# A post-norm decoder layer on one core: both batches share weights in the attention and one output projection

## The chip, the core and the metric

The kernel runs on one core of a Trainium2 chip. The time is that of one execution on the device, in microseconds (us). The kernel before ran three times: 1895.61, 1897.80 and 1900.67 us, median 1897.8. A further execution was recorded by the hardware profiler; its own time, from the first to the last instruction, is called the span.

The engines that appear below: TensorE (PE; its weight loads are shown apart as PEld), VectorE (DVE), ScalarE (ACT), GpSimd (POOL) and SyncE (SP), which issues nearly all transfers. Each engine works through its own instructions in order, and a transfer that waits for its room holds back those behind it on SP.

## The reference

Two batches of 512 tokens with 1024 features each go through one layer (cut to what is computed):

```python
def attention(x, wq, wk, wv, wo):           # 32 query heads, 8 key/value heads, 128 wide
    q, k, v = x @ wq.T, x @ wk.T, x @ wv.T  # split into heads, 4 query heads share one k and v
    s = q @ k.T / sqrt(128)                 # masked: j <= i and i - j < 128
    return (softmax(s) @ v) @ wo.T          # 4096 features back to 1024

def cross(x, ctx):                          # ctx: 2 x 1024 x 1024
    fake = lambda a, s, z: (clip(round(a / s + z), 0, 255) - z) * s
    return fake(x, s1, z1) @ fake(ctx, s2, z2)

def ffn(x):                                 # ternary weights, 2752 wide
    inter = silu(x / 128 @ w_gate.T) * (x / 128 @ w_up.T)
    q = int8(trunc(clip(inter * 128, -128, 127)))
    return int8(trunc(clip(q @ w_down.T * 128, -128, 127)))

x = layernorm(x + attention(x))
x = layernorm(x + cross(x, ctx[b]))
x = layernorm(x + ffn(x))
```

## The kernel before

**Arithmetic.** The f32 products are done with one level of Strassen and Winograd's form: seven products of half-size blocks in place of eight, with sums of blocks made by DVE. A product of f32 with 256 columns is two PE instructions, which follow each other 216 ns apart, so 0.432 us in the profile. A pair of heads of one batch costs 28 such products in `strassen` (L132), 12.1 us. The sums of the weights' blocks are made by `strassen_left` (L112 to L115: four DVE operations on 128x512), those of the activations, once for a batch, by `strassen_right`.

**Attention.** `attention` goes through 16 groups: the eight key/value heads of batch 0, then the eight of batch 1. A group takes three pairs of projections: key and value, then query heads 0 and 1, then 2 and 3. So each weight pair is loaded (L240) and summed twice, once for each batch. While a group's four tiles of 128 tokens are attended to, the projections of the next group run between the steps, `STEPS = 6` calls of `other` for one tile. A tile ("row" below) is: two score matmuls (`ps`, L338), copies and mask (L348 to L352), the row's maximum (L359), `exp` (L362), its reciprocal (L367), the multiplication that makes the weights (L368), transposes on PE (`pt`, L374), copies, and the matmuls `o` (L395 to L398), whose result goes into `factors` (L401). `keep` makes the Strassen sums of `factors` and stores them in DRAM as `kept` (L424).

**Background.** Generators stand in lists and are advanced a step at a time by `in_attention`: `ahead` makes the weights' sums of the output projection and the FFN and stores them in DRAM (`wo_sums`, `sums`); from batch 1 on, `behind` runs the output projection of batch 0 and `aside` its cross tokens.

**Output projection.** `project_out(b)` is made once for each batch. Its 56 steps go through seven products k in the order 1, 2, 6, 7, 4, 5, 3, and for each k through eight groups g. One step takes the seven sums of `kept` (`ol`, 448 KB, L483) and the weights (`or`, 512 KB, L490; from `wo` for k up to 3, from `wo_sums` above), makes four DVE sums of the latter (`right_sums`, L502, L503, L504 and L507: 128x256) and does seven products of 256 columns (L563, 3.02 us). After g = 7 of a k, `read` adds the products to the residual rows `xres` (L524 to L530). The loads for the weights are issued three steps ahead, those of `ol` two ahead.

**Cross attention.** `Cross.context(b)` reads the context in eight tiles of 512 KB: a load into the one buffer of `b_raw` (L635), three DVE operations (`quantise`, L615, L620, L621), and one ACT operation (`whole`, L625) which writes the tile as bf16. `constants` loads four parameters ahead of this (L597) and takes reciprocals of them. `tokens(b)` does the layernorm of four tiles, their product with the context, and the second layernorm.

**FFN.** 22 units of 128 features for batch 0, then 22 for batch 1. Between the units of batch 0 stand the output projection of batch 1 (1020 to 1334 us), its context and its tokens.

**Order.** The tile framework keeps each engine's instructions in the order of the program unless a planner moves them; `keep_in_program_order` pins one. PSUM before: two banks for projections, four for `y`, one for scores, one for transposes.

Of the kernel before, what the change touches and what calls it, by code (L numbers as in the profile page):

```python
# [18 lines left out]
P = 128  # L19
B = 2  # L20
# [26 lines left out]
SLOT = {1: 0, 2: 1, 3: 6, 4: 3, 5: 4, 6: 5, 7: 2}  # L47

# [39 lines left out]
def strassen_right(nc, pool, x, name):  # L88


    factors, steps = strassen_right_steps(nc, pool, x, name)
    for step in steps:
        step()
    return factors


def strassen_right_steps(nc, pool, x, name):

    b11, b12, b21, b22 = (x[:, ts(k, KH), ts(n, NH)] for k in range(2) for n in range(2))
    t = pool.tile([P, 4, KH, NH], F32, tag="t", name=name)  # L100
    t1, t2, t3, t4 = (t[:, k] for k in range(4))
    less = lambda *which: lambda: nc.vector.tensor_tensor(*which, ALU.subtract)
    return (b11, b21, b22, t4, t1, t2, t3), (less(t1, b12, b11), less(t2, b22, t1), less(t3, b22, b12), less(t4, b21, t2))
# [15 lines left out]
def strassen(nc, spaces, work, left, right, outs, name, sums=None):  # L119

# [11 lines left out]
    def bank(k):  # L135
        return spaces[k // 2].tile([P, NH], F32, tag="p", name=f"prod{k}_{name}")

    if sums is None:
        sums = [work.tile([P, NH], F32, tag=f"st{k}", name=f"st{k}_{name}", bufs=1) for k in range(3)]
    p1, u2, u3 = sums  # L140
# [5 lines left out]
    nc.vector.tensor_tensor(u2, two, p1, ALU.add)  # L146
    yield
    roomy = spaces[0] is not spaces[1]
    if roomy:
        three = bank(2)  # L150
        product(three, 5, True)
        yield
# [4 lines left out]
    nc.vector.tensor_tensor(u3, two, p1, ALU.add)  # L157
    yield
    if roomy:
        nc.vector.tensor_tensor(c22, like(three), like(u3), ALU.add)  # L160
        four = bank(3)
        product(four, 4, True)
        nc.vector.tensor_tensor(c21, like(four), like(u3), ALU.add)
        yield
    else:
        three = bank(2)
        product(three, 5, True)
        nc.vector.tensor_tensor(c22, like(three), like(u3), ALU.add)
        yield
        product(two, 4, False)  # L170
        nc.vector.tensor_tensor(c21, like(two), like(p1), ALU.add)
        yield
    product(three, 3, False)
    nc.vector.tensor_tensor(c12, like(three), like(u2), ALU.add)
# [6 lines left out]
class Background:  # L181
# [20 lines left out]

    def drain(self):
        while self.queue:
            for _ in self.queue.pop(0)[0]:
                pass


def attention(nc, tc, consts, xbuf, tpool, wpool, ps_p, ps_y, dram, kept, complete, between):

# [3 lines left out]
    with ExitStack() as ctx:  # L217
# [8 lines left out]
        groups = [(b, g) for b in range(B) for g in range(NKV)]  # L226
        STEPS = 6

        PAIRS = 1 + G // 2
        order = [(b, g, j) for b, g in groups for j in range(PAIRS)]  # L230
        weights, lefts, right = {}, {}, {}

        def load_weight(n):
            if n >= len(order):
                return
            _, g, j = order[n]
# [6 lines left out]
        def prepare(n):  # L243
            if n < len(order):
                lefts[n] = strassen_left(nc, tc, wpool, weights[n], f"s_{n}")

        def load_x(b):
            xT = xbuf.tile([P, KC, N], F32, tag=f"x{b}", name=f"xT{b}")
# [9 lines left out]
            return xT  # L258

        weights[0] = wpool.tile([P, 2, KC, P], F32, tag="w", name="w_0")  # L260
        x0 = load_x(0)
        load_weight(1)

        qT, kT, vT, v, vd = {}, {}, {}, {}, {}

        def project_first(outs):

            ps = [ps_p.tile([P, N], F32, tag="p", name=f"first{h}") for h in range(2)]
            for c in range(KC):

                for k, part in enumerate((ts(0, NH), ts(1, NH)) if c == 0 else (slice(None),)):
                    for h in range(2):
                        nc.tensor.matmul(  # L273
                            ps[h][:, part], weights[0][:, h, c], x0[:, c, part],
# [4 lines left out]
            load_weight(2)  # L279
            prepare(1)  # L280
            right[0] = strassen_right(nc, tpool, x0, "t_0")

        def project(n):

            b, g, j = order[n]
            if j == 0:
                c1 = kT[b, g] = kvpool.tile([P, N], F32, tag="kT", name=f"kT_{n}")
                c2 = vT[b, g] = kvpool.tile([P, N], F32, tag="vT", name=f"vT_{n}", bufs=1)
# [4 lines left out]
            if n == 0:  # L293
                project_first((c1, c2))
                yield
                return
            outs = [c[:, ts(half, c.shape[1] // 2)] for c in (c1, c2) for half in range(2)]
            for k, _ in enumerate(strassen(nc, (ps_p, ps_y if b == 0 else ps_p), work, lefts.pop(n), right[b], outs, n)):
                if k == 4:
                    prepare(n + 1)  # L300
                elif k == 6:
                    load_weight(n + 2)
                yield LUMP if k == 4 else None

        def transpose_v(b, g):
# [3 lines left out]
            v[b, g] = kvpool.tile([P, TPB, P], F32, tag="v", name=f"v_{b}_{g}")  # L309
            nc.scalar.copy(v[b, g], ps)  # L310
            vd[b, g] = kvpool.tile([P, TPB - 1, P], F32, tag="vd", name=f"vd_{b}_{g}")
            nc.vector.tensor_tensor(vd[b, g], v[b, g][:, 1:], v[b, g][:, : TPB - 1], ALU.subtract)

        def pieces(m):

            b, g = groups[m]
            for j in range(PAIRS):
                yield from project(m * PAIRS + j)
                if j == 0:
                    transpose_v(b, g)  # L320
                    yield
# [109 lines left out]
        for _ in pieces(0):  # L431
            pass
        pending, late = None, []
        for m, (b, g) in enumerate(groups):
            if m + 2 == NKV:
                x1 = load_x(1)
            if m + 1 == NKV:

                right[1], late = strassen_right_steps(nc, tpool, x1, "t_1")
                late = list(late)  # L440
                for _ in range(2):
                    late.pop(0)()
            rest = pieces(m + 1) if m + 1 < len(groups) else iter(())
            for i in range(TPB):

                def other():
                    lump = next(rest, None)
                    if late:
                        late.pop(0)()
                        lump = LUMP  # L450
                    between(b, g, i, lump, keeping)

                s = scores(b, g, i, other)
                weigh(pending, other)
                pending = b, g, i, s
                for _ in range(STEPS - 2):
                    other()
            for _ in rest:
                pass
# [4 lines left out]
def project_out(nc, tc, b, xres, spaces, psum, kept, complete, wo_d, sums, x_d, begun):  # L464

    respool, stream = spaces  # L470
    LAST = NKV - 1


    grow = {1: (True, ((0, 1), (1, 0), (1, 1))), 2: (False, ((0, 0),)), 6: (True, ((0, 1),)),
            7: (False, ((1, 1),)), 4: (False, ((1, 0),)), 5: (True, ((1, 1),)), 3: (False, ((0, 1),))}
    steps = [(k, g) for k in grow for g in range(NKV)]
    lefts, rights, factors = {}, {}, {}

    def load_left(n):
        if n < len(steps):  # L480
            k, g = steps[n]
            lefts[n] = stream.tile([P, 7, P], F32, tag="left", name=f"ol_{b}_{n}", bufs=3)
            nc.sync.dma_start(out=lefts[n], in_=kept[:, g, SLOT[k]])  # L483

    def load_right(n):
        if n < len(steps):
            k, g = steps[n]
            rights[n] = stream.tile([P, 2, 2, HQ], F32, tag="right", name=f"or_{b}_{n}")
# [3 lines left out]
    def right_sums(n):  # L492

# [6 lines left out]
        t = stream.tile([P, 3, HQ], F32, tag="sums", name=f"ot_{b}_{n}", bufs=2)  # L500
# [14 lines left out]
    while b and not begun[0]:  # L515
        yield
# [3 lines left out]
    banks = [psum.tile([P, 2, HQ], F32, tag="p", name=f"y{k}_{b}") for k in range(4)]  # L520

    places = {1: (0, 0), 6: (0, 1), 7: (1, 0), 2: (2, 0), 3: (2, 1), 4: (3, 0), 5: (3, 1)}
    order = list(places)

    def read(k):
        w = stream.tile([P, 4, HQ], F32, tag="right", name=f"yw_{b}_{k}")
        p1, u4, u2, u3 = (w[:, j] for j in range(4))
        q1, q6, q7, q5 = banks[0][:, 0], banks[0][:, 1], banks[1][:, 0], banks[3][:, 1]
# [6 lines left out]
        grown = banks[2], banks[3]  # L535
# [4 lines left out]
        for n, (h, e) in enumerate(grow[k][1]):  # L540
            for q in range(2):
                block = x[:, 2 * h + q, ts(e, HALF)].rearrange("p (e c) -> p e c", e=2)
# [6 lines left out]
    for n, (k, g) in enumerate(steps):  # L549
        while n + 2 < len(steps) and (b, steps[n + 2][1], "kept") not in complete:  # L550
            yield
        if n == NKV - 4:
            while b and (b - 1, "tokens") not in complete:
                yield
            x = respool.tile([P, TPB, D], F32, tag="xres", name=f"xres{b}")
            for i in range(TPB):
                nc.sync.dma_start(out=x[:, i], in_=x_d[ts(b * TPB + i, P), :])
                xres[b * TPB + i] = x[:, i]
        left, mine, sums_now = lefts.pop(n), factors.pop(n), following
        for part in (order[:4], order[4:]):  # L560
            for j in part:
                bank, half = places[j]
                nc.tensor.matmul(  # L563
                    banks[bank][:, half], left[:, SLOT[j]], mine[j],
                    start=grow[k][0] and g == 0 and half == 0, stop=g == LAST, skip_group_check=True,
                )
# [665 lines left out]
```

## Time and profile before

| | |
|---|---|
| runs, us | 1895.61, 1897.80, 1900.67; median 1897.8 |
| span of the profiled execution, us | 1894.7 |
| mean granted PE clock | 0.998 |
| PE instructions (matmuls, transposes) | 8678 |
| bytes moved by DMA | 416.88 MB, 220 GB/s mean |
| read from / written to HBM | 318.77 MB / 96.47 MB |
| longest wait of PE | 3.6 us, for the first tile of `xT` at the start |

How it is read: an engine's busy time is given beside its share of the span. A line of 40 digits shows the busy share of each fortieth of the span in tenths, 9 for 90% or more; PEclk is the clock granted to PE in tenths of full speed. The chain that ended last is the chain of work followed back from the last instruction. A group of instructions is given as line, engine, operation, output<-inputs, partitions x elements. For a transfer the profile shows where it was issued and when it landed.

### The profile page before, as it was taken

The numbers are of one execution on the slowest core, as the hardware profiler recorded it, in microseconds if no ns is written. First come the engines' busy times: TensorE is split into PE (matmuls) and PEld (weight loads), VectorE is DVE, ScalarE is ACT, GpSimd is POOL, SyncE is SP. The second block draws the span as 40 slices with busy tenths as digits, with TensorE's granted clock in tenths as the row PEclk, the third lists the DMA queues.
The fourth block names the chain that finished last, engine by engine and source line by source line (L and its number), as shares of the span: only waits on it lengthen the run. The fifth ranks groups of instructions, "written<-read, shape, count | busy, mean of one in ns | idle before, by whom it ended". The sixth has DMA issues, their size and how long they took to land.

```text
span 1894.7 us, 24665 instructions
## 1 busy us (share of the span) xinstructions
PE 1871.1 (99%) x8678; PEld 1547.8 (82%) x8678; DVE 1370.2 (72%) x3021; ACT 563.5 (30%) x1571; POOL 13.7 (1%) x32
## 2 busy tenths in 40 slices
PE   9999999999999999999999999999999999999997
PEld 6888888878888888888777888888787778888885
DVE  4678888887777676768787667766876787655657
ACT  1334433332221221233543111212233254321224
POOL 0000000000000000000000000000000000000000
PEclk9999999999999999999999999999999999999999
DMA  8478888777888888856367777766344245643431
GB/s 310 169 264 287 289 279 279 269 246 252 281 297 275 283 276 290 280 189 211 122 211 277 270 274 251 268 234 221 122 150 149 86 150 178 200 138 132 167 130 45
DMA packets 183323, 416.88 MB, mean 220 GB/s; under 512 B 16672, under 2 KB 93728, under 8 KB 183200
## 3 DMA queue, kind: packets, MB, share of 16 engines
q1 hardware_dynamic: 181760, 412.94, 63.3%
q10 hardware_dynamic: 1440, 2.36, 0.4%
q8 instruction: 69, 1.13, 0.2%
q14 instruction: 54, 0.44, 0.1%
HBM read 318.77 MB, written 96.47 MB: 219 GB/s over the span
## 4 chain that ended last, share of the span: by engine, by line
PE 86%; DVE 7%; DMA 3%; ACT 2%; issue 1%; SPq 0%; DVEq 0%; ACTq 0%
PE prod L132 51%; PE y L563 16%; PE d L819 7%; PE ps L338 3%; PE o L397 2%; PE o L398 2%; PE m L687 1%; PE pt L374 1%; PE first L273 1%; PE o L395 1%; ACT s L362 1%; DMA ol<-kept 1%; PE rest L811 1%; DMA wd<-in_wd_dram 1%; DVE factors L409 0%
## 5 line engine op out<-in xcount | busy, mean ns | idle before, releaser
L563 PE MATMUL y<-or,ol 128*128 128x256 f32 x896 | 243.4, 379 | 1.3 <-DMA ol<-kept 1.2
L563 PEld LDWEIGHTS y<-or,ol 128*128 128x128 f32 x896 | 169.1, 190 | 27.9 <-issue 3.2
L563 PE MATMUL y<-ot,ol 128*128 128x256 f32 x672 | 184.3, 383 | 1.4 <-DVE ot L507 1.1
L132 PE MATMUL prod<-xT,w 128*128 128x256 f32 x752 | 182.9, 380 | 0.1
L132 PE MATMUL prod<-t,w 128*128 128x256 f32 x752 | 177.0, 379 | 0.0
L132 PE MATMUL prod<-t,s 128*128 128x256 f32 x752 | 176.9, 379 | 0.1
L132 PE MATMUL prod<-x2T,wgu 128*128 128x256 f32 x672 | 160.2, 379 | 0.0
L132 PEld LDWEIGHTS prod<-t,s 128*128 128x128 f32 x752 | 140.3, 190 | 23.6 <-issue 5.5
L132 PEld LDWEIGHTS prod<-xT,w 128*128 128x128 f32 x752 | 139.4, 190 | 24.3 <-issue 6.7
L132 PEld LDWEIGHTS prod<-t,w 128*128 128x128 f32 x752 | 140.1, 190 | 23.2 <-issue 6.2
L132 PE MATMUL prod<-t,wgu 128*128 128x256 f32 x672 | 158.2, 379 | 0.0
L132 PE MATMUL prod<-t,sgu 128*128 128x256 f32 x672 | 155.7, 379 | 0.7 <-ACT g L154 0.5
L563 PEld LDWEIGHTS y<-ot,ol 128*128 128x128 f32 x672 | 124.7, 190 | 27.5 <-DVE ot L507 6.2
L132 PEld LDWEIGHTS prod<-t,sgu 128*128 128x128 f32 x672 | 127.2, 190 | 19.4 <-ACT g L154 0.9
L132 PEld LDWEIGHTS prod<-t,wgu 128*128 128x128 f32 x672 | 127.3, 190 | 18.6 <-issue 0.5
L132 PEld LDWEIGHTS prod<-x2T,wgu 128*128 128x128 f32 x672 | 127.4, 190 | 17.9 <-issue 0.5
L362 ACT ACTIVATE s<-s,top 128x128 f32<-128x128 f32 x256 | 99.6, 391 | 37.8 <-DVE top L359 37.0
L819 PE MATMUL d<-hi,act 128*128 128x512 f32 x256 | 108.1, 422 | 0.0
L348 ACT COPY s<-ps 128x128 f32<-128x128 f32 x192 | 39.5, 231 | 229.0 <-PE ps L338 228.9
L833 DVE TENSOR_TENSOR acc<-d,acc 128x512 f32<-128x512 f32 x104 | 71.6, 691 | 44.6 <-PE d L819 44.1
L819 PE MATMUL d<-lo,act 128*128 128x512 f32 x256 | 101.3, 396 | 0.0
L157 DVE TENSOR_TENSOR st<-prod,st 128x256 f32<-128x256 f32 x89 | 37.6, 422 | 81.2 <-PE prod L132 81.0
(220 smaller groups left out, 2985.8 us busy)
## 6 DMA issues: line engine op xcount, KB each, us to landing
kept<-factors SPq DMA_DIRECT2D x112, 448.0 KB, 3.5
ol<-kept SPq DMA_DIRECT2D x112, 448.0 KB, 5.2
w<-in_wq_dram SPq DMA_DIRECT2D x64, 512.0 KB, 4.7
or<-wo_sums SPq DMA_DIRECT2D x64, 512.0 KB, 5.1
sgu<-sums SPq DMA_DIRECT2D x42, 768.0 KB, 6.4
or<-in_wo_dram SPq DMA_DIRECT2D x48, 512.0 KB, 4.5
wgu<-in_wgu_dram SPq DMA_DIRECT2D x42, 512.0 KB, 3.9
wd<-in_wd_dram SPq DMA_DIRECT2D x42, 512.0 KB, 3.6
```

The source lines that it names most:

```text
L132: nc.tensor.matmul(ps, left[k - 1][:, c, :], right[k - 1][:, c, :], start=start and c == 0, stop=c == KH - 1, skip_group_check=True)
L157: nc.vector.tensor_tensor(u3, two, p1, ALU.add)
L273: nc.tensor.matmul(ps[h][:, part], weights[0][:, h, c], x0[:, c, part], start=c == 0 and k == 0, stop=c == KC - 1, skip_group_check=True,)
L338: nc.tensor.matmul(ps[:, k, cut // BLOCK : G + 1].rearrange("p d w -> p (d w)"), qT[b, g][:, G * i + c].rearrange("p h w -> p (h w)"), kT[ ...
L348: nc.scalar.copy(s[:, c, c * BLOCK :], ps[:, k, : G - c].rearrange("p d w -> p (d w)"))
L362: nc.scalar.activation(s[:, h, :], s[:, h, :], AF.Exp, bias=top[:, h : h + 1], scale=QSCALE, accum_out=total[:, h : h + 1],)
L374: nc.tensor.transpose(ps[:, :, ts(c, BLOCK)], s[:, c, :], ident)
L397: nc.tensor.matmul(ps, v[b, g][:, i - 1, :], both, start=True, stop=False)
L398: nc.tensor.matmul(ps, vd[b, g][:, i - 1, :], cur, start=False, stop=True)
L563: nc.tensor.matmul(banks[bank][:, half], left[:, SLOT[j]], mine[j], start=grow[k][0] and g == 0 and half == 0, stop=g == LAST, skip_group_ ...
L819: nc.tensor.matmul(ps, act[:, ts(i, P)], half[:, part], start=start and k == 0, stop=stop and k == len(parts) - 1)
L833: nc.vector.tensor_tensor(acc[t][:, ts(e, HALF)], ps, acc[t][:, ts(e, HALF)], ALU.add)
```

## The change

**Attention.** The loop goes over the eight heads outside and the two batches inside. `sets` lists for each head which pair of which batch is projected when: pair 0 of both, pair 1 of batch 0, pair 2 of batch 0, and then, while batch 0's rows are attended to, pairs 1 and 2 of batch 1. A weight pair is loaded once and summed once and stays until both batches have used it. Both batches' activations are loaded at the start, and both sums of them made there. The number of calls for a row is 5 for batch 0 and 8 for batch 1 (`STEPS = (5, 8)`). Of the background only `ahead` remains in the attention (a step for three calls, before four), and in the last group (batch 1, head 7) steps of the output projection for every second call.

**Output projection.** One `project_out` serves both batches. Its 63 steps: k = 1 for g = 0 to 6 of batch 0, then of batch 1, then g = 7 of both; then k = 6, 7, 4, 5, 3, 2, each with eight g for both batches. A step's `or` and its four sums serve both. PSUM has seven banks for it. The `ol` have six buffers (before three). The first `read`, after k = 1, feeds four blocks of the output for each batch in place of three.

```diff
-    steps = [(k, g) for k in grow for g in range(NKV)]
+    steps = [(1, g, (0,)) for g in range(LAST)] + [(1, g, (1,)) for g in range(LAST)] + [(1, LAST, (0, 1))]
+    steps += [(k, g, (0, 1)) for k in grow if k != 1 for g in range(NKV)]
...
+        mine, sums_now = factors.pop(n), following
+        for b in bs:
+            left = lefts.pop((n, b))
+            for part in (order[:4], order[4:]):
+                for j in part:
+                    bank, half = places[b][j]
...
+            if b == bs[-1]:
+                following = right_sums(n + 1)
+                next(following)
+                load_right(n + 3)
+                load_left(n + 2)
```

**After the attention.** The pools of the cross part and the residual rows are opened only when the attention has ended, in room that the attention used. The eight residual tiles are loaded one after the other, and both contexts and the tokens of the first share run between the steps of the output projection:

```diff
+    for share, pool in ((1, resid), (0, first_resid)):
+        for t in SHARES[share]:
+            xres[t] = pool.tile([P, D], F32, tag=f"xres{t}", name=f"xres{t}")
...
+    for _ in residual():
+        pass
+    behind.add(cross.context(0), 2)
+    behind.add(cross.context(1), 2)
+    behind.add(cross_tokens(0))
+    for n, lump in enumerate(output):
+        if n == 60:
+            for u in range(2):
+                left[u] = load_factors(nc, wpool, gate_up, u, u)
+        if not lump:
+            behind.step()
+    behind.drain()
+    outer.close()
```

**Shares.** Tokens and FFN no longer go by batches. `LATE` is tiles 2 and 3 of both batches, `EARLY` tiles 0 and 1 of both. The late share's tokens come first, then its FFN, in which the early share's tokens run; then the early share's FFN.

```diff
+LATE = tuple(b * TPB + i for b in range(B) for i in (2, 3))
+EARLY = tuple(b * TPB + i for b in range(B) for i in (0, 1))
+SHARES = (LATE, EARLY)
```

**Smaller edits.** `strassen` always uses four banks of one pool (before, two variants); the sums of the FFN's output lie in a tile of `tpool`; the bf16 context tiles lie in pairs in one tile; `Turns` alternates between two PSUM pools for the tokens in the FFN. Lines move: L563 becomes L559, L483 L482, L490 L489, L635 L632, L625 L622, L597 L594.

## The prediction, written before the changed kernel was run

> **What bounds the kernel now.** The page's first parts come first: busy time by engine, the span in 40 slices, the shares of the chain that ended last. Then the four stages in a table of windows.
>
> ```profile
> PE 1871.1 (99%) x8678; PEld 1547.8 (82%) x8678; DVE 1370.2 (72%) x3021; ACT 563.5 (30%) x1571; POOL 13.7 (1%) x32
> PE   9999999999999999999999999999999999999997
> PEclk9999999999999999999999999999999999999999
> PE 86%; DVE 7%; DMA 3%; ACT 2%; issue 1%; SPq 0%; DVEq 0%; ACTq 0%
> ```
> ```profile
> 0.00:430.00 430.00, 424.67 (x1985) 346.57 (x1986) 327.61 (x770) 147.06 (x568) 5.64 (x18) 1.00 0.77 266
> 430.00:1030.00 600.00, 596.05 (x2833) 491.78 (x2832) 443.34 (x1070) 178.06 (x630) 4.20 (x8) 1.00 0.73 248
> 1030.00:1550.00 520.00, 517.42 (x2358) 427.09 (x2357) 377.73 (x761) 122.74 (x190) 1.94 (x3) 1.00 0.58 200
> 1550.00:1894.70 344.70, 332.94 (x1507) 282.34 (x1506) 221.51 (x422) 115.67 (x184) 1.93 (x3) 0.99 0.42 143
> ```
>
> The columns are stage, length, busy us of PE, weight loads, DVE, ACT and POOL, granted clock, DMA share and GB/s. TensorE is the bound everywhere: idle 5.3, 4.0, 2.6 and 11.8 us in the four stages, at full clock. The first idle holds 3.6 us before the first matmul, the last some 11.5 us after the last one. I also took the PE's instructions start to start and compared each gap with the median of its kind: the excess over medians is 31 us of the whole span, 0.2 to 1.8 us in most stretches of 50 us and 6.5 us at 950 to 1050, where the attention of batch 1 ends. So whatever is saved on other engines is worth nothing unless it shortens those 31 us, and every microsecond in which PE is left without work is lost in full.
>
> **What the change leaves alone.** The order of instructions after the change holds as many of every kind of PE instruction as before. Shared weight loads save 32 of 64 wq loads, some 16 of 30 wk and wv loads, 49 of 112 `or` loads, 92 (23 x 4) left sums of 0.68 us and 196 (49 x 4) right sums of 0.42 us: about 145 us of DVE, and 97 transfers of 512 KB. DVE is 72% busy and the DMA share is 0.42 to 0.77, both behind PE: worth 0. The cover is the PE work itself; where that cover ends is what follows.
>
> **Attention, +2.** A row's softmax (end of the second score matmul to end of the normalising multiply, L338 to L368) took 4.2 to 5.8 us in rows where nothing queued, 4.46 typically. Before, PE had at least 7.5 us of other work in between in all rows but the last few, which had 4.74 and stalled there. After, in the steady groups the thinnest rows (batch 0, last tile) have 5.5 to 6.4 us: enough, with DVE's queue not always. In the last group covers fall to 2.1 and 2.7 us, with 0.5 us between transposes and the `o` matmuls: four or five waits of some 2 us, 9 us in all. Against that, the 6.5 us of excess at before's own end of attention goes. 9 - 6.5 = +2.5; I take +2. Bounds: all rows covered -8 (the 6.5 and a little of the steady excess), 32 thin rows short by 0.4 us on top, +15.
>
> **Hand-over to the output projection, +20.** Here SP's queue decides. Before, it looked like this (PE, then SP at the same place):
>
> ```profile
> 1016.17 1.02 PE L398 MATMUL o<-cur,vd 128*128 128x512 f32 x2
> ```
> ```profile
> 1019.69 4.73 SPq L424 DMA_DIRECT2D kept<-factors  x5
> 1024.51 0.41 SPq L490 DMA_DIRECT2D or<-in_wo_dram  x1
> 1025.62 0.32 SPq L483 DMA_DIRECT2D ol<-kept  x1
> ```
>
> The last `o` matmul ends at 1017.19; call that T0. The last five stores of `kept` are issued from T0+2.5 to T0+7.2 and land 3.5 us later (row kept<-factors). Before, FFN matmuls fill PE meanwhile. After, PE has only 48 output matmuls that need nothing from them (48 x 0.432 = 20.7 us) and the 14 of the last k=1 step (6.05): T0+26.8 if nothing waits. In SP's order after the change, step 11's two operands follow the stores; they land at about T0+13, PE wants them at T0+8.8: 4.2 us. Then stand the four residual loads of the late tiles (the first reuses `factors`' room, so waits for all five stores, T0+10.7), four parameter loads (landing 4.3) and the first context load; the operands of steps 12 to 14 come after them. DVE is in order too: the reciprocal of the parameters (here at about T0+18.3) and the quantising of the first context tile stand ahead of step 8's right sum, which is ready at T0+22, while PE would want it at 13.9: 8 us more. The next three context loads each hold SP until ACT has released the one buffer, with the operands of the next steps behind each. By hand the k=1 steps end at T0+46.6 in place of T0+26.8: 20 us. Bounds: only the 4.2 and half the rest, +10; +25 if every landing takes the 6 to 7 us of the slower rows (xres<-in_x_dram 7.0).
>
> **Context tiles, +14.5.** One tile takes this, before (SP, then DVE, then ACT):
>
> ```profile
> 1231.40 0.33 SPq L635 DMA_DIRECT2D raw<-in_ctx_dram  x1
> 1232.17 3.72 SPq L490 DMA_DIRECT2D or<-wo_sums  x2
> 1236.43 0.32 SPq L483 DMA_DIRECT2D ol<-kept  x1
> 1238.95 0.33 SPq L635 DMA_DIRECT2D raw<-in_ctx_dram  x1
> ```
> ```profile
> 1235.48 0.80 DVE L615 TENSOR_SCALAR raw<-raw,inv,par 128x1024 f32<-128x1024 f32 x1
> 1236.32 0.69 DVE L620 TENSOR_SCALAR raw<-raw 128x1024 f32<-128x1024 f32 x1
> 1237.05 0.69 DVE L621 TENSOR_SCALAR raw<-raw 128x1024 f32<-128x1024 f32 x1
> ```
> ```profile
> 1237.78 1.15 ACT L625 ACTIVATE a<-raw,down 128x1024 bf16<-128x1024 f32 x1 [6.40 <-DVE raw L621]
> ```
>
> Load, three DVE operations (1235.48 to 1237.74), one ACT operation, next load: 7.55 us from 1231.40 to 1238.95, the fastest cycle of the trace; others took 9.6 to 24 us, hidden by FFN or attention matmuls on PE. After the change one context load stands in SP's queue per output step, ahead of the next steps' operands, and a step of both batches is 14 x 0.432 = 6.05 us of PE. So each of the 16 tiles costs 7.5 - 6.05 = 1.45 us, once the operands loaded ahead are used up. The steps from 15 on carry 12 tiles: 4 x 1.45 = 6 for the first series, 8 x 1.45 = 11.6 less about 3 us of stock refilled in between, 8 for the second: 14.5. Bounds: +5, landing at the minimum of 3.2 (3.2 + 2.26 + 1.15 = 6.6; 0.55 x 12 less the stock), +25 at 8.5 us a cycle. The trace shows no other price for a load, so no gain is in it. Rate is not the limit: a step's 1.44 MB and 0.52 MB of context in 6.05 us are 325 GB/s, and windows of 5 us moved up to 419 GB/s.
>
> **First read of the sums, +4.5.** k=1 now feeds four blocks: per batch on DVE 3 x 0.36 + 2 x 0.64 + 8 x 0.61 = 7.2 us. Both batches' 14.4 us stand ahead of step 15's last right sum, and PE has one 6.05 us step and some stock: a wait of about 4.5. Bounds 0 (the stalls above let DVE catch up) and +9 (14.4 less one step).
>
> **Tokens and the boundary to FFN, +2.** Cross tokens of the late tiles run in the last two k; the last read must free a bank before FFN's products: 1 to 2 us. Bounds -2 and +8, from before's excess per 50 us and one late tile. **FFN, -2.** Fewer ACT table loads, half the background: bounds -5 (all of its excess but the tail) and +3.
>
> **Sum.** 2 + 20 + 14.5 + 4.5 + 2 - 2 = 41. The profiled execution spans 1894.7; 1935.7. The median of the runs, 1897.8, is 3.1 above that span: forecast **1939**. The bounds taken together as independent (roots of squared distances, 18 below, 20 above) give **1921 to 1959** for this case alone.
>
> [...] The trace grants PE 0.5 until 8.3 us, though matmuls start at 3.6, and 0.5 again from 1885.7, 2.8 us after the last one ended. [...]
>
> **Rivals.**
> *Faster, 1889.* SP runs ahead: the order allows the context load to land while operands for three more steps are already in SBUF, so the stalls never reach PE, and before's 6.5 us go: 1894.7 - 6.5 - 2 + 3.1 = 1889. It decides if a context cycle is at most 6.05 us, that is a landing of at most 2.64, and residual and parameters land by T0+9. Against it: the shortest of those landings is 3.2, and the stores alone land at T0+10.7.
> *No change, 1899.* Only the 4.2 us and a part of the 8 appear (+10), the read and the context hide behind stock, and -6.5 - 2 pay them: 1894.7 + 1.5 + 3.1 = 1899. For it: excess in before's busiest stretches never passed 4 us per 50; against it: they had FFN matmuls beside them.
> *Much slower, 1973.* The context cycle is 9.6 us, the next fastest of the trace, as DVE's sums stand between its operations: 16 x 2.1 = 34 more.
>
> **How the numbers follow.** Chances: forecast case 0.67, faster 0.11, no change 0.09, much slower 0.13. Within 0.3% (5.7 us) can't be told from no change here. The range leaves out the faster case and the upper half of the much slower one: 1895 to 1966. Of the no-change case some 0.06 is within the bound and 0.03 above: faster 0.11, same 0.06, slower 0.83.
>
> **What would show it.** Right: PE waits on L559 for `ot` and `or` of 4 to 10 us right after attention, and some 12 of 1 to 2 us between there and 80 us later; SP waiting at L632 for ACT's L622 in most context loads; DVE busy about 1225 us. The attention step is wrong if waits for the multiply exceed 15 us in all or are absent. All is wrong if PE's idle time after attention is under 10 us; then the loads were issued earlier than I read from the order.

## The result and the profile after

The changed kernel takes 1956.2 us (median of four runs, 1954.9 to 1956.7) against 1897.6 (the three runs of before and a fourth, 1897.4): a ratio of 1.0305, interval 1.029 to 1.0319, so 58.6 us slower. That is the forecast's sign, and inside its range (1895 to 1966); the forecast of 1939 was 17 us short. The profiled execution spans 1954.0 us. The page's parts that answer to those of before:

```profile
PE 1882.2 (96%) x8668; PEld 1550.2 (79%) x8678; DVE 1266.3 (65%) x2737; ACT 543.6 (28%) x1556; POOL 13.7 (1%) x32
PE   7999999999999999967899999999999999999997
PEclk9999999999999999979999999999999999999999
PE 78%; DVE 11%; DMA 6%; ACT 3%; issue 1%; SPq 0%; DVEq 0%; ACTq 0%
```

PE has the same work (8678 weight loads) and 3% less of the span is busy. The gap is in two places of the 40: the first digit, and the 6, 7 and 8 just behind the end of the attention, where the clock falls too. In the chain that ended last, PE lost eight points, DVE and DMA gained seven. DVE's busy time is 104 us shorter, and nothing of that shows in the time. A table of windows cut at the stages (attention to 750, its last head to 833, output projection with the context, its rest, FFN; columns as before):

```profile
0.00:750.00 750.00, 735.03 (x3472) 604.45 (x3473) 490.21 (x1181) 244.12 (x1002) 9.29 (x25) 1.00 0.60 207
750.00:833.00 83.00, 77.61 (x354) 59.75 (x353) 49.41 (x122) 31.41 (x134) 0.52 (x1) 0.98 0.57 208
833.00:1001.00 168.00, 133.19 (x556) 107.66 (x557) 102.69 (x211) 20.44 (x21) 0.00 (x0) 0.92 0.74 258
1001.00:1225.00 224.00, 222.13 (x1055) 185.12 (x1058) 129.14 (x307) 19.78 (x39) 0.00 (x0) 1.00 0.63 212
1225.00:1954.00 729.00, 714.21 (x3238) 593.22 (x3240) 494.84 (x918) 227.89 (x361) 3.87 (x6) 1.00 0.40 141
```

PE is idle 35 us of the 168 in the third row, at a granted clock of 0.92; before, no stage but the tail lost more than 5.3. The waits of PE, and those of DVE from 833 to 1000 us (who waits, for what, total, times, longest):

```profile
PE y L559 <- DVE ot L505: 17.5, 6, 9.3
PE first L263 <- DMA xT<-in_xT_dram: 11.7, 1, 11.7
PE y L559 <- DMA ol<-kept: 11.1, 8, 4.6
PE y L559 <- DVE ot L501: 5.6, 5, 2.2
```
```profile
DVE raw L612 <- DMA raw<-in_ctx_dram: 42.4, 12, 4.8
DVE inv L596 <- DMA par<-in_s_dram: 12.3, 1, 12.3
```

PE waits for right sums (`ot`), and DVE, which makes them, waits at the same time for context tiles and parameters. The second line of PE's list is 3.6 us in the profile before.

The hand-over, from the timelines of SP and then DVE:

```profile
835.54 4.54 SPq L434 DMA_DIRECT2D kept<-factors  x5
840.18 0.68 SPq L489 DMA_DIRECT2D or<-in_wo_dram  x1
840.91 1.03 SPq L482 DMA_DIRECT2D ol<-kept  x1
843.01 1.77 SPq L1124 DMA_DIRECT2D xres<-in_x_dram  x4
844.83 0.45 SPq L594 DMA_DIRECT2D par<-in_s_dram  x1
...
848.35 0.33 SPq L632 DMA_DIRECT2D raw<-in_ctx_dram  x1
```
```profile
853.46 0.16 DVE L596 RECIPROCAL inv<-par 128x1 f32<-128x1 f32 x1 [12.27 <-DMA par<-in_s_dram]
...
855.92 0.81 DVE L612 TENSOR_SCALAR raw<-raw,inv,par 128x1024 f32<-128x1024 f32 x1 [0.80 <-DMA raw<-in_ctx_dram]
...
858.10 0.42 DVE L505 TENSOR_TENSOR ot<-or,ot 128x256 f32<-128x256 f32 x1
```

The right sum of the last line was ready to be made long before; it stands behind two things that come by DMA, and PE, whose list shows the 9.3 us, stands behind it.

To size the terms I use the prediction's own measure: each PE instruction's distance to the next, less the median of its kind ("excess"). Steps are counted by products, since the order lets products of neighbouring steps pass each other. T0 is the end of the last `o` matmul, 833.3 us.

| | before | after | difference | predicted |
|---|---|---|---|---|
| start, to the first matmul | 3.6 | 11.7 | +8.1 | none |
| attention to T0 (before: to 1022) | 17.2 | 18.4 | +1.2 | +2 |
| T0 to the end of k=1 | | 25.7 | +25.7 | +20 |
| next two steps | | 9.6 | +9.6 | +4.5 |
| steps 17 to 31, context | | 13.2 | +13.2 | +14.5 |
| all the rest (before: from 1022) | 13.2 | 17.0 | +3.8 | 0 |
| tail, and the sum of the medians | | | -2.4 | |
| span | 1894.7 | 1954.0 | +59.3 | +41 |

Each column is one profiled execution. How far such a figure scatters can be read from the experiments below, where a stretch has the same instructions as here: the attention has 18.4 to 25.0 us of excess, the hand-over (T0 to the end of k=1) 25.7 to 27.8, steps 17 to 31 12.0 to 18.0, all the rest 13.3 to 17.0. Differences of a few microseconds in one row are not shown to be more than that.

### The profile page after: what moved, and what is told of

It reads as the page before. It is cut to its first block, busy times and chain, and to the rows that moved or that the text cites. A ratio compares the mean times of both kernels' runs of the same rounds, so it can differ in the third digit from the quotient of the medians.

```text
span 1954.0 us, 24145 instructions
## 1 busy us (share of the span) xinstructions
PE 1882.2 (96%) x8668; PEld 1550.2 (79%) x8678; DVE 1266.3 (65%) x2737; ACT 543.6 (28%) x1556; POOL 13.7 (1%) x32
## 4 chain that ended last, share of the span: by engine, by line
PE 78%; DVE 11%; DMA 6%; ACT 3%; issue 1%; SPq 0%; DVEq 0%; ACTq 0%
PE prod L131 49%; PE y L559 11%; PE d L818 7%; PE ps L348 3%; DMA raw<-in_ctx_dram 3%; PE o L407 2%; PE o L408 2%; PE pt L384 1%; PE m L686 1%; PE first L263 1%; ACT a L622 1%; DMA out_dram<-fin_x 1%; PE o L405 1%; DVE raw L612 1%; DVE xres L524 1%
## 5 line engine op out<-in xcount | busy, mean ns | idle before, releaser
L559 PE MATMUL y<-or,ol 128*128 128x256 f32 x896 | 230.2, 384 | 12.8 <-DMA ol<-kept 11.1
L559 PE MATMUL y<-ot,ol 128*128 128x256 f32 x672 | 183.1, 391 | 23.2 <-DVE ot L505 17.5
L559 PEld LDWEIGHTS y<-or,ol 128*128 128x128 f32 x896 | 170.0, 192 | 41.8 <-issue 11.6
L131 PE MATMUL prod<-t,w 128*128 128x256 f32 x752 | 172.8, 379 | 0.0
L559 PEld LDWEIGHTS y<-ot,ol 128*128 128x128 f32 x672 | 128.0, 195 | 49.8 <-DVE ot L505 19.4
L137 DVE TENSOR_TENSOR st<-prod,st 128x256 f32<-128x256 f32 x178 | 75.1, 422 | 129.9 <-PE prod L131 129.7
L131 PE MATMUL prod<-t,wgu 128*128 128x256 f32 x672 | 154.0, 379 | 0.0
L131 PEld LDWEIGHTS prod<-t,wgu 128*128 128x128 f32 x672 | 127.5, 190 | 18.4
L348 PEld LDWEIGHTS ps<-kT,qT 128*128 128x128 f32 x512 | 80.1, 190 | 16.9 <-DVE s L362 5.5
```

The lines of the kernel that those rows point to most:

```text
L131: nc.tensor.matmul(ps, left[k - 1][:, c, :], right[k - 1][:, c, :], start=start and c == 0, stop=c == KH - 1, skip_group_check=True)
L137: add = lambda out, y, z: nc.vector.tensor_tensor(out, y, z, ALU.add)
L348: nc.tensor.matmul(ps[:, k, cut // BLOCK : G + 1].rearrange("p d w -> p (d w)"), qT[b, g][:, G * i + c].rearrange("p h w -> p (h w)"), kT[ ...
L559: nc.tensor.matmul(bank[:, half], left[:, SLOT[j]], mine[j], start=grow[k][0] and g == 0 and half == 0, stop=g == LAST, skip_group_check=True,
```

## The experiments

The theory: PE's work is unchanged and was the bound, so the time grows by what PE waits, and it waits because on two in-order queues the operands of the output projection stand behind loads that come late. Rivals: transfers are simply at their rate; SP's queue alone is at fault; DVE's amount of work sets the pace. Each kernel below is the changed kernel with the edits named, and from "All together" on each takes over the edits of the one before; ratios are to the kernel before on the same chip.

**The start.** The scratch tiles of the masks come to lie at the other end of SBUF.

```diff
-    with tc.tile_pool(name="masks", bufs=1) as masks:
+    with tc.tile_pool(name="masks", bufs=1, side="right") as masks:
```

> The changed kernel with one edit: the scratch tiles of the masks are put at the other end of SBUF, so that the first tile of x no longer takes their room. Theory: the first transfer of x waits for GpSimd and VectorE to be done with the masks, issued at 5.0 us in place of 0.5; without that PE starts at about 3.5 us, not 11.7, and the time falls by 8 us to about 1948. Rival: it is the larger traffic at the start (x of batch 1, weights), then the start stays at about 11 us and the time at 1956.

Measured 1950.0 us (1947.8 to 1957.9), ratio 1.0269 [1.0247, 1.0291]. PE's first wait, in its list of waits:

```profile
PE first L263 <- DMA xT<-in_xT_dram: 4.1, 1, 4.1
```

The cause is shown: with the room free, the start is as before. Before the change the `xbuf` pool lay behind others; in the changed kernel it is the first to be opened after the masks' pool is closed and takes its place, so the first load of x waits for the engines that build the masks. Of 7.6 us some 6 reach the median; the profiled execution, the slowest of the four, has 5.7 us more excess in the attention.

**Parameters early.** The four loads and the operations on them become a generator of the attention's background.

```diff
-        if b == 0:
-            self.constants()
...
+    ahead.add(cross.constants(few))
     ahead.add(sum_output_weights())
```

> The changed kernel with the four parameter loads and the few VectorE operations on them moved from the hand-over into the attention's background. Theory: the 9.4 us wait of PE for step 9's right sum at 849 to 858 falls by at most 4, as the first context tile (here landed at 855.6) is still ahead of that sum on VectorE: the time falls by 2 to 6 us. Rival: the parameters alone are what is late (landing 8.6 us), then 8 us or more go.

Measured 1953.3 us, 1.0286 [1.0261, 1.0311]: -3, as the theory had it, though this interval and the changed kernel's overlap. The longest wait for `ot` falls from 9.3 to 7.2 us. DVE's wait there is still 12.2 us and ends with the landing of the first context tile, at 854.2 us.

**Two context buffers.**

```diff
-        ctx.enter_context(tc.tile_pool(name="b_raw", bufs=1, reuse_waits="tile")),
+        ctx.enter_context(tc.tile_pool(name="b_raw", bufs=2, reuse_waits="tile")),
```

> The changed kernel with two buffers for context tiles. Theory: the cycle of load, three VectorE operations and ScalarE (7.3 to 8.5 us for steps of 6.05) is what paces steps 17 to 31; with two buffers the load overlaps the rest, these steps fall to about 6.3 us and 10 to 13 us go there, and some of the hand-over: 1956 to about 1940. Rival: the traffic or the order of SP's queue paces them, then the steps stay over 6.8 us and less than 4 us go.

Measured 1941.8 us, 1.0234 [1.0213, 1.0255]: -14. The excess of steps 17 to 31 falls from 13.2 to 4.7 us, 8.5 where 10 to 13 were expected, at the same traffic and the same order of the other loads. DVE's wait for context tiles falls from 42.4 us:

```profile
DVE raw L612 <- DMA raw<-in_ctx_dram: 17.4, 8, 6.4
```

So the transfer rate does not pace these steps.

**Context loads from ScalarE's queue.**

```diff
-            nc.sync.dma_start(out=r, in_=self.ctx_d[b, ts(c, P), :])
+            nc.scalar.dma_start(out=r, in_=self.ctx_d[b, ts(c, P), :])
```

> The changed kernel with the context loads issued from ScalarE's queue in place of SP's, one buffer as before. Theory that the cycle itself paces VectorE, and through it the right sums: steps 17 to 31 stay at about 7 us, and only what stood behind a waiting context load on SP comes earlier, -3 to -12 us in all. Rival that SP, held by each context load's wait for ScalarE (36.3 us in 14 waits), is what keeps the operands late: steps fall to 6.05 us, and 25 us or more go.

Measured 1958.5 us, 1.0316 [1.0297, 1.0335]: no gain at all, less even than the theory's -3; steps 17 to 31 have 16.5 us of excess. Over the same stretch DVE's list of waits keeps its first line:

```profile
DVE raw L612 <- DMA raw<-in_ctx_dram: 43.7, 11, 7.1
```

In the changed kernel SP's own queue had waited for ScalarE at these loads:

```profile
SPq L632 <- ACT a L622: 36.3, 14, 8.9
```

Without that wait PE is held as before, so it was not what held PE. It is DVE's order, as the changed kernel itself shows at one tile (DVE, then PE):

```profile
966.98 0.81 DVE L612 TENSOR_SCALAR raw<-raw,inv,par 128x1024 f32<-128x1024 f32 x1 [4.79 <-DMA raw<-in_ctx_dram]
967.83 0.69 DVE L617 TENSOR_SCALAR raw<-raw 128x1024 f32<-128x1024 f32 x1
968.55 0.69 DVE L618 TENSOR_SCALAR raw<-raw 128x1024 f32<-128x1024 f32 x1
969.16 0.42 DVE L500 TENSOR_TENSOR ot<-or 128x256 f32<-128x256 f32 x1
969.62 0.42 DVE L501 TENSOR_TENSOR ot<-or,ot 128x256 f32<-128x256 f32 x1
```
```profile
970.10 0.70 PE L559 MATMUL y<-ot,ol 128*128 128x256 f32 x2 [2.21 <-DVE ot L501]
```

DVE idles 4.8 us until the tile has landed, does its three operations, then the sums; PE gets its operand at 970.1 and had waited 2.2 us.

**Context later.** It starts when k=1 has been read.

```diff
+                if b == bs[-1]:
+                    complete.add(("read", k))
...
-        if not lump:
+        if not lump and ("read", 1) in complete:
             behind.step()
```

> The changed kernel with the context (its parameters too) started only after the first read of the sums, so that the four context loads and their VectorE work leave the hand-over. Theory: they hold SP and VectorE there; PE's excess from the last o matmul to the end of k=1 falls from 25.7 us to about 10 (the late ol of 4.6 us and its clock stay), the four tiles cost some 6 us later: 1956 to about 1945. Rival: the stores of kept, the residual loads and their traffic hold the operands, then the excess stays over 20 us and the time within 4 us of 1956.

Measured 1958.2 us, 1.0322 [1.0305, 1.034]. The theory's first half holds: the excess up to the end of k=1 falls from 25.7 to 12.9 (about 10 expected), and that of the next two steps by 4.3. Its second half fails: steps 17 to 46 go from 13.3 to 30.2, where 6 more were expected. Sixteen tiles with one buffer cost PE about 2 us each there (30.2 / 16); DVE's wait for them was 47.6 us. The expectation had priced only the four tiles that move; why the other twelve cost more as well is not shown.

**The same sums twice.** Three of four left sums of each weight pair are made again, with the same result.

```diff
+    if name.startswith("s_"):
+        nc.vector.tensor_tensor(s1, a21, a22, ALU.add)
+        nc.vector.tensor_tensor(s2, s1, a11, ALU.subtract)
+        nc.vector.tensor_tensor(s4, a12, s2, ALU.subtract)
```

> The changed kernel doing three of the four left sums of each weight pair of the attention a second time (72 more VectorE operations of 0.68 us, 49 us, with the same result). Theory that saved VectorE work is worth nothing while PE has other work: 0, at most +4 us. Rival that VectorE's queue sets the rows' pace: +10 us or more.

Measured 1955.3 us, 1.0312 [1.0295, 1.033], DVE busy 1307.0 us in place of 1266.3: no change. So 41 us more or less of DVE's work in the attention are worth nothing. What order is worth, the next experiment shows.

**SP's order at the hand-over.** On top of the later context: parameters early, residual loads two at a time between the steps, and `ol` loaded up to four steps ahead.

```diff
-                load_left(n + 2)
+                load_lefts(n + 1)
...
-    for _ in residual():
-        pass
+    rows = residual()
...
+        if n >= 3:
+            next(rows, None)
```

> e5 with three more edits at the hand-over: parameters early as in e2, the residual loads two for a step in place of all eight at once, and the ol operands of the single-batch steps loaded four steps ahead in place of two. Theory: with SP's order mended PE's excess from the last o matmul to the end of k=1 falls to under 6 us, the time by some 6 us under e5, to about 1938. Rival: the transfer rate is the limit there (residual rows and operands of 3.02 us steps at once), then it stays at 10 us or more whatever the order.

Measured 1947.5 us, 1.027 [1.0255, 1.0285]. The excess from T0 to the end of k=1 is 6.5 us, from 12.9 with the later context alone and 25.7 in the changed kernel. Against the later context alone about the same bytes go in that stretch (12.4 MB for 12.9), so half of those 12.9 us was order and not rate. They go at 375 GB/s in place of 327, with the 16 DMA engines busy 0.98 of the time in place of 0.87, so the 6.5 us that are left may be rate; no run separates that. The time is 10.8 us under that of the later context alone, where 6 were expected; the expected 1938 was missed because the later context itself came out 13 us above its expectation. Steps 17 to 46 still have 31.5 us, as the context has one buffer here.

**All together.** On top of that: the masks, two context buffers, and at the end of each k the next step's right sums ahead of the read.

```diff
+                        if g == LAST:
+                            following = right_sums(n + 1)
+                            next(following)
+                            next(following, None)
```

> e7 with the masks' scratch moved (e1), two context buffers (e3), and the right sums of the step after a first read put ahead of that read on VectorE. Theory: the terms add: start -6, hand-over -20, the first read 9.6 to about 3, context 13 to about 5: 1956 to about 1913, still over the kernel before, since the end of the attention and the tail are as they were. Rival: what is mended in one place is lost in the next, then it stays over 1925.

Measured 1912.1 us, 1.0084 [1.0069, 1.0099]; 1913 was expected. Steps 17 to 46 have 3.2 us of excess, 31.5 in the previous experiment. With the context late the second buffer is worth most of these 28 us; how much of them the sums put ahead of the read hold is not shown. The two steps behind the first read still have 5.7.

**The first read in two parts.** Only what reads PSUM stays at the end of k=1; the 16 adds into the residual rows follow during k=6, and each batch's read has scratch of its own for it.

```diff
+        if k == 1:
+            later.extend((blocks, part) for part in grow[k][1])
+            return
...
+        if k == 6 and g < 4:
+            for _ in range(2):
+                blocks, part = later.pop(0)
+                blocks(*part)
```

> e8 with the first read in two parts: only the operations that read PSUM stay at the end of k=1, for both batches; the 16 adds into the residual rows follow in the first four steps of k=6. Theory: PE's waits after k=1 are for VectorE's 14.4 us of reads (yw, 4.7 us in e8, and the right sums behind them), the excess of the first two steps of k=6 falls from 5.7 us to about 1: 1912 to about 1907. Rival: the banks are freed no earlier, or the adds hold the next right sums: within 2 us of 1912.

Measured 1909.6 us, 1.0054 [1.0036, 1.0072]. The two steps' excess falls from 5.7 to 1.7, as expected, and that of steps 17 to 31 from 2.6 to 0.7; 5.3 us more in the early attention of the profiled execution hide a part in its span.

**Cover for batch 0's last row.**

```diff
-        last = b and g == NKV - 1
+        last = g == NKV - 1 and (b or i == TPB - 1)
```

> e9 with the output projection's first steps begun one row earlier, in the last row of batch 0's last head, which has no cover. Theory: the waits of 0.9 to 2.2 us for that row's softmax go, and as much is missing later only in part, -1 to -3 us against e9. Rival: the same 17 half steps are merely spread thinner and the later rows wait as much more: no change against e9.

Measured 1903.0 us, 1.0028 [1.0018, 1.0038]: -6.6, more than twice what was expected. The last head's excess goes only from 10.0 to 9.4, and the hand-over's from 7.1 to 3.6; the rest is 1.9 us in the early attention, which this edit doesn't touch. That the waits of that row alone were worth it is not shown.

**Thinner background, and one sum earlier.** One background step for four calls in place of three; then the last right sum of the next single-batch step is put out half a step earlier.

```diff
-        elif credit[0] >= 3 and ahead.queue:
-            credit[0] -= 3
+        elif credit[0] >= 4 and ahead.queue:
+            credit[0] -= 4
...
+                    if len(bs) == 1:
+                        next(following)
```

> e10 with a background step for four calls of the attention in place of three (its last store would move from 510 us to some 680). Theory: the waits of the attention before its last head (10.4 us in e10) come partly from background VectorE work and transfers that stand in the rows' way, 2 to 5 us go: 1903 to about 1899, level with the kernel before within 0.3%. Rival: they come from the rows' cover alone: no change.

> e11 with the last right sum of the next single-batch step put out half a step earlier, ahead of the sums for kept on VectorE. Theory: the wait of 2.4 us at the hand-over is for this sum behind them; it goes, -1 to -3 us against e11. Rival: VectorE is late there as a whole, then something else is late by as much: no change. A version under the kernel before by more than 0.3% (below 1892) is expected by neither.

Measured 1899.9 us, 1.0013 [1.0003, 1.0022], for the first, as expected; its attention has 14.5 us of excess in place of 19.8, a difference within the scatter of unchanged code, so where the gain lies is not shown. With both: 1898.4 us, 1.0004 [0.9995, 1.0013]; the hand-over goes from 5.8 to 3.7. Each interval overlaps the one before it. The two lines for this last kernel that answer to those of the changed one, page and DVE's waits from 821 to 990 us:

```profile
PE 1869.7 (99%) x8668; PEld 1546.9 (82%) x8678; DVE 1265.2 (67%) x2737; ACT 542.9 (29%) x1556; POOL 13.7 (1%) x32
```
```profile
DVE raw L648 <- DMA raw<-in_ctx_dram: 10.6, 8, 1.8
```

PE is back at 99%, with DVE still 105 us below the kernel before. PE's excess is 36.2 us in all, 84.0 in the changed kernel and 30.4 in the kernel before. No version here is faster than the kernel before: with most of the stalls taken out, sharing the weight loads and sums is worth nothing that can be measured.

## Why the prediction was right, and where it was short

**The bound.** Right, and the point on which all else rests: PE's work is the same, so the saved 51 MB and 104 us of DVE bring nothing. The 145 us worked out for DVE were right: added one by one, its operations take 1533.9 us before and 1392.7 after, 141 less; busy time counts once what overlaps, and successive operations overlap (sums that take 0.42 us start 0.34 us apart). The bound is shown from both sides, by the repeated sums (41 us more of DVE busy, no change) and by the last kernel, which keeps the savings and ends level.

**The sum.** It gave +41 for the span, and +59.3 came. The 18 us between them are 8.1 of the start, 5.7 of the hand-over, 5.1 of the first read and 3.8 of the rest, less 0.8, 1.3 and 2.4 in the other rows. So 8.1 us of what carried the time close to the forecast's own upper bound of 1959 come from a term that the prediction did not have.

**The start** is the step that was missing: the sum has no term for it, since the places that tiles take in SBUF were not weighed. +8.1 us. In the traces ScalarE issues the first load of x at 5.3 us, behind a wait, and at 0.8 us in the kernel before, without one.

**Attention** +1.2 measured, +2 predicted; with the scatter of 18.4 to 25.0 us the size is not settled. The place is: 9.9 us lie behind 750 us, in the last head, where 9 were forecast, and the many thin rows before it have 8.5 in all.

**Hand-over** +25.7, with +20 predicted and +25 as the bound. Its events came as worked out: a late `ol` of 4.2 us (4.6), then a right sum for 8 us (9.3). What was mis-sized: the parameters landed after 7.7 to 8.6 us, not the 4.3 of the row before, with four residual loads of 512 KB ahead of them, and the clock fell: 16 PE instructions at half speed, 0.21 us more each, are 3.4 of the 5.7 us beyond the forecast. The sum has no term for that. That the order was the cause was shown by the later context and SP's mended order, which left 6.5 us.

**First read** +9.6 in place of +4.5, just past its bound of +9. It holds two context tiles as well; with the right sums ahead and the read split, 1.7 are left (there the context has moved away too).

**Context** +13.2 in place of +14.5, the cycle 7.4 to 8.9 us in steps 17 to 31 where 7.5 was taken. The size was right within the scatter (the row holds ten tiles, the forecast twelve), and its path in part wrong: the prediction had the load hold SP and the operands behind it. Moved off SP it cost the same. The step holds PE through DVE, which waits for the tile ahead of the right sums. The second buffer, which shortens that wait, took most of it away.

**Tokens, boundary and FFN** +3.8 in place of 0; in the other runs the same code has 13.3 to 16.4 us for the 17.0 here, so this is within the scatter.

**The rivals.** The faster one asked for a context cycle of at most 6.05 us; none was under 7.3. The one of no change had the read and the context hidden behind operands loaded ahead; both show, with 9.6 and 13.2 us. The much slower one, 1973 with 9.6 us a cycle, missed by 17 us, as the forecast did on the other side; cycles of 11.0, 11.4 and 11.0 us stand among the first eight tiles.

**The signs.** PE's waits on L559 for `ot` came, those for `or` did not (it was `ol`); SP waited for ScalarE at 14 of 16 context loads; DVE was busy 1266 us, not 1225.

## What to carry to other kernels

With one engine busy 99%, as here, sharing loads and sums of other engines gained nothing (1898.4 us for the last kernel, 1897.1 beside it for the kernel before), while what was reordered to share them uncovered that engine (35 us idle between 833 and 1001 us): look in the new order for each queue's waiting instruction and for what stands behind it. A load into a single buffer, whose consumer stands in the same in-order queue as the bound engine's operands, held that engine where its cycle, landing included, was longer than the bound engine's step (7.4 to 8.9 us against 6.05); a second buffer cost one line here and gained 14 us, and moving the load to another queue gained nothing. A pool that was opened in the room of a closed one waited for what used that room, at the start of the kernel too: the first load of x was issued at 5.3 us in place of 0.8.

## What the runs showed of the hardware that was not expected

**The clock fell in the middle of the kernel.** In the kernel before, the record of the clock has it at full from 8.6 us and at half from 1886.0, each 0.3 us later than the prediction read; the matmuls of 256 columns up to 7.2 us follow each other 427 ns apart. In the changed kernel the clock is at full from 15.7 us, with 427 ns between most of the matmuls ahead of that, and falls to half at 793.89 (in the attention's last head), 845.09, 868.98, 903.12 and 971.38 us; it stays there for 17.07 us from 845.09 on, for 3.41 us each of the other four times, and falls again at 1947.6, behind the last matmul. Between 833 and 1001 us 30 PE instructions of 256 columns took 427 ns in place of 216, 6.3 us more. The spell from 845.09 on begins within the first of the two long waits (4.57 and 9.35 us), outlasts the second, and has nine of these instructions; the other three have seven, 3 us, each, and followed waits of 1.9, 2.3 and 2.2 us, which ended at 867.7, 902.1 and 970.1. Waits of 2.1 and 3.1 us, which ended at 883.4 and 891.1, left the clock at full. In a table of windows of 1 us (PE is idle in the first):

```profile
901.00:902.00 1.00, 0.00 (x0) 0.00 (x0) 1.00 (x4) 0.00 (x0) 0.00 (x0) 1.00 0.00 0
902.00:903.00 1.00, 0.87 (x4) 0.80 (x5) 0.97 (x4) 0.00 (x0) 0.00 (x0) 1.00 0.00 0
903.00:904.00 1.00, 1.00 (x5) 0.79 (x4) 0.97 (x3) 0.00 (x0) 0.00 (x0) 0.56 0.85 242
904.00:905.00 1.00, 1.00 (x4) 0.81 (x3) 0.97 (x2) 0.00 (x0) 0.00 (x0) 0.50 0.90 319
```

Here the granted clock drops a microsecond after work has begun again. A wait of 1.9 us had a fall behind it and one of 3.1 us had none, so the length of a wait alone did not decide; what did is not shown.

**Small loads behind large ones.** Four parameter loads of 0.5 KB took 7.7 to 8.6 us to land behind four of 512 KB, and 3.5 to 5.0 in the kernel before behind seven of 256 KB. In both the first of them landed just after the last large one ahead of it: at 853.4 us after 852.6, and at 21.4 after 21.1.
